# Seam of layers 0 and 1 batch by batch, and layer 1's scatters one a stage

## The chip, the cores and the metric

The kernel runs on one core of one Trainium2 chip. Its time is the device time of one execution in microseconds (us). The kernel before takes 1791.88 us in the median of three runs (1789.32 to 1793.81). The names of the engines are those of the profile: PE does matmuls and transposes (PEld loads their weights), DVE vector work, ACT activations and copies, POOL vector work and the indirect DMAs that it issues itself, SP issues the other DMAs.

## The reference, cut to what matters

A batch of 4 sequences of 512 tokens with 128 channels goes through four layers. In each, `x = x + s * silu(f)`, where `s` comes from a mixer and `f` from an expert network, and both read the normalized input.

```python
xn = layernorm(x)
s = mamba_block(xn)                # layer 0: selective scan, 256 inner channels, 16 states
g = silu(moe0(xn))                 # 8 experts, dense, weighted by the top 2
x = x + s * g                      # <- end of layer 0
xn = layernorm(x)                  # <- start of layer 1
s = layernorm(causal_attention(xn) @ w_proj + b_proj + xn) * gamma + beta   # 16 heads of 8
g = silu(moe1(xn))                 # 4 usable experts of 704 hidden units, top 2
x = x + s * g
# layers 2 and 3 follow in the same form
```

The two lines with arrows are the seam. Layer 1's attention looks only within a sequence, and a norm only at one token, so batch 0 of layer 1 needs nothing of batches 1 to 3. The routing of `moe1` is over all 2048 tokens: a token's place among those of its expert depends on all tokens before it.

## The kernel before, in words

A batch is 512 tokens, four rows of 128 tokens on the partitions (`NC` = 16 such chunks in all). `x`, `s` and `acc` hold all of them as `[128, 16, 128]`; `xnT` is the normalized input transposed, `[128 channels, 2048 tokens]`.

**Layer 0** (`layer0`, L573) runs a loop of 128 scans (L721 to L725) over 32 tiles of each batch. A step has the decay on ACT (L712, `dA`, made six steps ahead), the product `dBx` (L719) and the scan (L723) on DVE, the product with C on POOL (L725), and every four steps a sum over states on PE (L734). The experts' 32 steps, (expert, batch) in this order, lie between: the hidden matmul on PE (L558), GELU on ACT (L559), the output matmul on PE (L569), and the weighted add into `acc` on DVE (L519). The last expert's four steps finish `acc` for batches 0, 1, 2 and 3 one after the other. `back(b)` (L745 to L752) projects the scan's result of a batch into `s`; for the last batch this is the last work of the layer. `load_x` fetches `x` a second time near the end (L270), because four of its tiles serve as buffers of the scan.

**The seam**: `end_layer0` (L438) does one silu over all of `acc`, then `s = s * acc` and `x = x + s` in two halves. `begin_layer` (L431) takes `bn_stats` and `bn_aggr` of 16 chunks (L297, L298), one square root and reciprocal for all, 16 normalizes (L316), 16 transposes on PE (L323), and four copies into `xnT` (L324). POOL clears buffers of the attention meanwhile (L1701, L1707); SP loads the eight constant key blocks (L1704), then the attention's weights (L894, L896).

**Layer 1's attention** (`attention`, L882) runs in steps, one for each (batch, group of four heads, key block): 64 of them. Step k takes two score passes for a step 8 ahead (`first_pass`: PE L919 and L926, then the maximum of a row on DVE, L1026), and the two probability passes of its own (PE L919, exp on ACT L1057, and for the first 36 steps a causal mask on POOL, L1061). The matmuls with the values (`apply`, L1073) of step k - 1 stand between them. So steps -8 to -1 have score passes alone. `project(b)` (L962) makes queries, keys and values of a batch and splits q and k into bf16 parts; `spread(n)` (L1002) is 16 DMAs on SP that lay the parts of a group out for the passes. `shift` (L1028) sends the row maxima to the queries by four more DMAs.

**Routing** (`Routed.route`, L1200) is a generator. It takes the gate logits of all tokens (16 matmuls, L459), then some 40 small DVE operations, in which each token's two places in the experts' list are found, and then 32 scatters on POOL (L1298): chunk c of the rows goes to its first and to its second places in `xs` in HBM. After that `load` fetches two tiles' weights (L1311, 1.18 MB each, on POOL) and rows (L1317, on SP). Each scatter writes into the same `xs`, and in the order of instructions it waits for the semaphore of the scatter before it.

**What sets the order.** Within `tc.manual_schedule` an engine's instructions stay in the order in which the program makes them; the seam before is outside of it. The order in layer 1 is planned by `Places` (L334). Each attention step offers two stages (`place`, called in the middle and at the end of `step`). In a stage, due jobs go first (projections, shifts, ends of groups), then one stage of a due chain (`work`), and then, if a rule allows, one stage of the generator in `beside` (`aside`). What the generator yields says when it may go on:

```python
if self.needs == "free" or self.needs == "dve" and dve_left or self.needs is None and bank_left and (
    self.every or not second or not was
):
    self.aside()
```

`"free"` is any stage, `"dve"` the first of a step (and the second in every third step), and nothing means that a PSUM bank is needed. A chain that was served comes up again one step later (`gap=1`). `need(key)` runs a chain to its end at once. After step 35 (`PAUSE`) the rest of the routing is run, and then `routed.run` (L1342) does 19 tiles of experts, whose first hidden matmul is L1354.

`turn(b)` (L1406) is the seam's work for one batch, used so far behind layers 1 and 2: the product on POOL, the add, statistics and normalizes on DVE (`rows_norm`, L407, with Ln and Exp on ACT for the root), four transposes and a copy into `xnT`.

Of the kernel before, what the change touches and what calls it, by code (L numbers as in the profile page):

```python
# [11 lines left out]
F32 = mybir.dt.float32  # L12
BF16 = mybir.dt.bfloat16
I32 = mybir.dt.int32
AF = mybir.ActivationFunctionType
# [215 lines left out]
def kernel(ctx: ExitStack, tc: tile.TileContext, ap: dict):  # L231
# [34 lines left out]
    eps = cpool.tile([P, 1], F32, name="eps")  # L266
    dve.memset(eps, EPS)
# [23 lines left out]

    def norm_stats(src):

        st = small.tile([P, NC, 6], F32, tag="ln_st", name="ln_st")
        mv = small.tile([P, NC, 2], F32, tag="ln_mv", name="ln_mv")
        for c in range(NC):
            dve.bn_stats(out=st[:, c, :], in_=src[:, c, :])  # L297
            dve.bn_aggr(out=mv[:, c, :], in_=st[:, c, :])  # L298
        ve = small.tile([P, NC], F32, tag="ln_ve", name="ln_ve")
        dve.tensor_scalar(ve, mv[:, :, 1], EPS, None, ALU.add)  # L300
        sd = small.tile([P, NC], F32, tag="ln_sd", name="ln_sd")
        act.activation(sd, mv[:, :, 1], AF.Sqrt, bias=eps)
        r = small.tile([P, NC], F32, tag="ln_r", name="ln_r")
        dve.reciprocal(r, sd)

        t = small.tile([P, NC], F32, tag="ln_t", name="ln_t")
        dve.tensor_tensor(t, r, r, ALU.mult)
        dve.tensor_tensor(t, t, ve, ALU.mult)
        dve.tensor_scalar(t, t, -0.5, 1.5, ALU.mult, ALU.add)
        dve.tensor_tensor(r, r, t, ALU.mult)  # L310
        return mv, r

    def normalize(dst, src, stats=None, chunks=range(NC)):
        mv, r = stats or norm_stats(src)
        for c in chunks:
            dve.tensor_scalar(dst[:, c, :], src[:, c, :], mv[:, c, 0:1], r[:, c : c + 1], ALU.subtract, ALU.mult)  # L316
# [113 lines left out]

    def begin_layer(s):  # L431

        normalize(s, x)
        xnT = keep.tile([P, N], F32, name="xnT")
        transpose_chunks(xnT, s, NC)
        return xnT

    def end_layer0(s, y):  # L438

        act.activation(y, y, AF.Silu)  # L440
        half = NC // 2
        for h in range(2):
            cs = slice(h * half, (h + 1) * half)
            dve.tensor_tensor(s[:, cs, :], s[:, cs, :], y[:, cs, :], ALU.mult)
            dve.tensor_tensor(x[:, cs, :], x[:, cs, :], s[:, cs, :], ALU.add)
# [127 lines left out]
    def layer0(ctx0, mp, fp, s_out, acc):  # L573
# [31 lines left out]
        xnT = keep.tile([P, N], F32, name="xnT")  # L605
# [576 lines left out]
    class Routed:  # L1182
# [17 lines left out]
        def route(self):  # L1200

            rp, wp = self.rp, self.wp
# [93 lines left out]
            for c in range(NC):  # L1296
                for a in range(2):
                    pool.indirect_dma_start(  # L1298
                        out=self.xs[:, :], out_offset=self.at(a, c), in_=self.rows[:, c, :], in_offset=None,
                        bounds_check=TILES1 * SLOT1 - 1, oob_is_err=False,  # L1300
                    )
                    yield "free"
                    yield "free"
# [102 lines left out]
    def turn(b, s, y, xnT):  # L1406
# [4 lines left out]
        pool.tensor_tensor(sb, sb, yb, ALU.mult)  # L1411
# [273 lines left out]
    acc = keep.tile([P, NC, D], F32, name="acc")  # L1685

    with banks("l0", 0, True, bank=3, py=1, dBx=2, B=1, y=1):
        with tc.tile_pool(name="moe0", bufs=2) as fp, tc.tile_pool(name="mamba", bufs=1) as mp:
            with ExitStack() as ctx0:
                layer0(ctx0, mp, fp, s, acc)  # L1690
    end_layer0(s, acc)

    with banks("l1", 3, True, bank=1, py=1), tc.tile_pool(name="heads", bufs=1) as hp:
# [8 lines left out]
        for g in pads["k"]:  # L1702
            for t in g:
                nc.sync.dma_start(out=t, in_=ap["c_kb"])  # L1704

        for t in vaug:
            pool.memset(t[:, :, :, SUM : SUM + 1], 1.0)  # L1707
        xnT = begin_layer(s)

# [18 lines left out]
        with ExitStack() as to3, tc.manual_schedule(engines=engines):  # L1728
# [3 lines left out]
            with tc.tile_pool(name="moe1w", bufs=1) as wp:  # L1732
# [8 lines left out]
                a1 = attention(1, hp, None, xnT, pads, vaug, s, end1)  # L1741
                for _ in a1.first:
                    pass
# [91 lines left out]
```

## Time and profile before

| | |
|---|---|
| median of the runs | 1791.88 us |
| the profiled execution: its time, its span | 1787.83 us, 1786.1 us |
| mean granted PE clock | 0.835 |
| busy: PE, DVE, ACT, POOL | 1355.6, 1149.5, 954.2, 535.8 us |
| last matmul of layer 0 (L750) ends | 475.28 us |
| first projection of layer 1 (L968) starts | 491.81 us |
| first score matmul (L919) starts | 509.43 us |
| first mask (L1061, step 0) | 535.50 us |
| first and last scatter (L1298) start | 529.26, 646.65 us |
| first weights of the routed experts (L1311) | 648.59 us |
| first hidden matmul of the routed experts (L1354) | 669.76 us |

Times in the timeline count from the start of the span. A line of it gives start, length, engine, source line, operation, output and inputs, how many instructions were merged, and in brackets the idle time of the engine before it with what ended that. In the table by stages each engine has its busy time and the number of its instructions; PEclk is the granted clock as a share of full speed.

### The profile page before, as it was taken

The numbers are of one execution on the slowest core, as the hardware profiler recorded it, in microseconds if no ns is written. First come the engines' busy times: TensorE is split into PE (matmuls) and PEld (weight loads), VectorE is DVE, ScalarE is ACT, GpSimd is POOL, SyncE is SP. The second block draws the span as 40 slices with busy tenths as digits, with TensorE's granted clock in tenths as the row PEclk, the third lists the DMA queues.
The fourth block names the chain that finished last, engine by engine and source line by source line (L and its number), as shares of the span: only waits on it lengthen the run. The fifth ranks groups of instructions, "written<-read, shape, count | busy, mean of one in ns | idle before, by whom it ended". The sixth has DMA issues, their size and how long they took to land.

```text
span 1786.1 us, 22629 instructions
## 1 busy us (share of the span) xinstructions
PE 1355.6 (76%) x7845; PEld 690.0 (39%) x7845; DVE 1149.5 (64%) x2007; ACT 954.2 (53%) x1307; POOL 535.8 (30%) x513
## 2 busy tenths in 40 slices
PE   5588878887568889998687667876768876788771
PEld 2345545555333338886232122322313322233331
DVE  6378788787755653322586876567658799976322
ACT  3456656665325653222336767786884544365640
POOL 1236364554505651112543403114011101031223
PEclk8589989899757889999688878788888898898875
DMA  3567778488221132432212240311311211112112
GB/s 111 152 165 208 173 235 219 137 227 203 62 39 37 41 104 78 162 113 70 41 20 55 33 61 6 54 18 26 47 27 26 80 19 19 19 41 68 40 39 76
DMA packets 119923, 149.69 MB, mean 84 GB/s; under 512 B 14393, under 2 KB 80513, under 8 KB 118017
## 3 DMA queue, kind: packets, MB, share of 16 engines
q1 hardware_dynamic: 112848, 123.60, 29.6%
q0 software_dynamic: 6960, 24.65, 4.2%
q8 instruction: 62, 1.02, 0.2%
q14 instruction: 53, 0.43, 0.1%
HBM read 114.89 MB, written 16.01 MB: 73 GB/s over the span
## 4 chain that ended last, share of the span: by engine, by line
PE 41%; DVE 19%; ACT 16%; issue 10%; DMA 8%; POOL 3%; SPq 2%; another core or an unknown queue 1%; ACTq 0%; DVEq 0%; POOLq 0%
PE py L1073 6%; PE wide L919 6%; PE wide L1354 6%; PE bank L558 5%; ACT at L1057 5%; DMA rep<-ddd 3%; PE wide L926 3%; DVE nm L1026 3%; PE py L1334 3%; ACT ep L1021 3%; DVE den L1022 3%; PE py L569 2%; ACT dA L712 1%; PE wide L968 1%; DVE hs L723 1%
## 5 line engine op out<-in xcount | busy, mean ns | idle before, releaser
L1057 ACT ACTIVATE at<-wide 128x1024 f32<-128x1024 f32 (+3 forms) x384 | 352.6, 924 | 261.1 <-PE wide L926 170.2
L1026 DVE TENSOR_REDUCE nm<-wide 128x2 f32<-128x1024 f32 (+3 forms) x256 | 256.8, 1019 | 100.7 <-PE wide L926 86.9
L1073 PE MATMUL py<-at,vaug 128*32 128x512 f32 (+3 forms) x1536 | 235.7, 670 | 11.8 <-POOL at L1061 8.6
L725 POOL TENSOR_TENSOR hc<-hs,C 128x512 f32<-128x512 f32 x128 | 163.0, 1279 | 226.6 <-DVE hs L723 124.4
L1022 DVE TENSOR_REDUCE den<-ep 128x2 f32<-128x1024 f32 x128 | 155.4, 1217 | 114.3 <-ACT ep L1021 113.6
L919 PE MATMUL wide<-k,q 48*128 48x512 bf16 (+4 forms) x768 | 165.2, 407 | 78.2 <-ACT at L1057 43.4
L558 PE MATMUL bank<-xnT,w 128*128 128x512 f32 x256 | 142.0, 704 | 80.9 <-ACT h L559 53.6
L723 DVE TENSOR_TENSOR_SCAN hs<-dA,dBx 128x512 f32<-128x512 f32 x128 | 154.8, 1210 | 9.2 <-POOL hc L725 9.2
L1021 ACT ACTIVATE ep<-wide 128x1024 f32<-128x1024 f32 x128 | 132.8, 1037 | 43.5 <-PE wide L919 34.0
L926 PE MATMUL wide<-own_bf 128*128 128x128 bf16 x880 | 137.1, 243 | 0.0
L712 ACT ACTIVATE dA<-rep,A 128x512 f32<-128x512 f32 x128 | 86.7, 715 | 85.7 <-DMA rep<-ddd 47.7
L919 PE MATMUL wide<-q,k 63*128 63x512 bf16 (+3 forms) x512 | 100.4, 387 | 41.0 <-ACT at L1057 24.4
L569 PEld LDWEIGHTS py<-w,h 128*128 128x128 f32 x1024 | 120.2, 194 | 19.3 <-issue 9.8
L569 PE MATMUL py<-w,h 128*128 128x128 f32 x1024 | 121.8, 278 | 1.3 <-DVE acc L519 1.3
L558 PEld LDWEIGHTS bank<-xnT,w 128*128 128x128 f32 x256 | 54.3, 223 | 169.1 <-ACT h L559 75.8
L919 PEld LDWEIGHTS <-q 48*128 48x128 bf16 (+1 forms) x768 | 49.8, 96 | 162.3 <-issue 143.8
L1359 DVE TENSOR_TENSOR h<-h,wide 128x512 f32<-128x512 f32 x57 | 39.2, 688 | 110.2 <-ACT h L1357 110.2
L1354 PE MATMUL wide<-xT,w 128*128 128x256 f32 x456 | 108.4, 387 | 2.1 <-ACT h L1357 1.6
L559 ACT ACTIVATE h<-bank,cols 128x512 f32<-128x512 f32 x128 | 84.7, 687 | 33.9 <-PE bank L558 33.3
L919 PE MATMUL wide<-qr,kr 48*128 48x512 bf16 x256 | 60.7, 448 | 45.9 <-ACT ep L1021 40.8
L926 PEld LDWEIGHTS <-own_bf 128*128 128x128 bf16 x880 | 51.9, 100 | 110.6 <-issue 103.6
L919 PEld LDWEIGHTS <-k 63*128 63x128 bf16 x512 | 29.1, 94 | 166.3 <-issue 152.4
(324 smaller groups left out, 2157.8 us busy)
## 6 DMA issues: line engine op xcount, KB each, us to landing
rep<-ddd SPq DMA_DIRECT2D x128, 256.0 KB
dx<-ddd SPq DMA_DIRECT2D x80, 256.0 KB
x<-ddd SPq DMA_DIRECT2D x48, 256.0 KB
q<-parts SPq DMA_DIRECT2D x192, 48.0 KB
k<-parts SPq DMA_DIRECT2D x192, 48.0 KB
w<-in_f_w_dram SPq DMA_DIRECT2D x18, 256.0 KB
ddd<-dd POOLq DMA_DIRECT2D x8, 512.0 KB
w<-in_f_w_dram SPq DMA_DIRECT2D x32, 128.0 KB
```

The source lines that it names most:

```text
L558: pe.matmul(ph, w1[:, f * P : (f + 1) * P], self.xnT[:, tb * L : (tb + 1) * L], start=True, stop=True)
L569: pe.matmul(py[:, cs], h[:, f, cs], w2[:, f, :], start=(f == 0), stop=(f == 3))
L723: dve.tensor_tensor_scan(h, st[n]["dA"], st[n]["dBx"], 0.0, ALU.mult, ALU.add)
L725: pool.tensor_tensor(hc, h, batch[tiles[n][0]]["C"], ALU.mult)
L919: pe.matmul(ps[:, j, lo:hi], lhs[m][r, cs], rhs[m][r, lo:hi], start=True, stop=not own)
L926: pe.matmul(ps[:, j, cs], lhs_own, rhs_own, start=False, stop=True)
L1021: act.activation(e, ps, AF.Exp)
L1022: dve.tensor_reduce(s["den"][:, qc, 2 * m : 2 * m + 2], e, AX.X, ALU.add)
L1026: dve.tensor_reduce(s["nm"][:, qc, 2 * m : 2 * m + 2], ps[:, :, :hi], AX.X, ALU.max, negate=True)
L1057: act.activation(a[:, :, lo:], ps[:, :, lo:], AF.Exp)
L1073: pe.matmul(s["po"][32 * j : 32 * j + 32, lo:], vaug[b % 2][:, kc, 4 * g + j, :], a[:, j, lo:], start=kc == 0, stop=kc == 3,)
L1354: pe.matmul(ph[:, g, m * SLOT1 : (m + 1) * SLOT1], wk[:, f + g, m, :], self.x[k], start=True, stop=True)
```

## The change

The seam is taken apart by batches. Layer 0 ends with four silus on ACT, one for each batch. The seam's work of a batch is now `turn(b)`, as behind layers 1 and 2, each put in a chain of the planner; for batch 0 the product is on DVE, and `places.need((0, 0))` runs it at once, before the attention's first projection. Batches 1 to 3 come a stage at a time in the attention's first steps. `project` already asks for the end of the chain `(i - 1, b)` before it reads `xnT`. The routing waits, giving up stage after stage, until all four chains are over. In its loop of scatters one of the two yields is gone, so that a scatter is placed in each stage instead of every second. The eight loads of constant keys are now issued after the attention's two weights. The tile `xnT` is made once and shared by both layers. `norm_stats`, `normalize`, `begin_layer`, `end_layer0` and the tile `eps` are no longer used.

In the order of instructions that the build gives the changed kernel, silu 0 and 1 and the vector work of `turn(0)` stand among the last scans of layer 0 on ACT and DVE, and each Ln and each Exp of the four turns has a table load of its own in front of it. The engines' orders from the end of the first 36 steps on are those of before.

```diff
-    def begin_layer(s):
-        normalize(s, x)
-        xnT = keep.tile([P, N], F32, name="xnT")
-        transpose_chunks(xnT, s, NC)
-        return xnT
-    def end_layer0(s, y):
-        act.activation(y, y, AF.Silu)
-        half = NC // 2
-        for h in range(2):
-            cs = slice(h * half, (h + 1) * half)
-            dve.tensor_tensor(s[:, cs, :], s[:, cs, :], y[:, cs, :], ALU.mult)
-            dve.tensor_tensor(x[:, cs, :], x[:, cs, :], s[:, cs, :], ALU.add)
...
         def route(self):
+            while not places.over.issuperset((0, b) for b in range(B)):
+                yield "free"
             rp, wp = self.rp, self.wp
...
                         out=self.xs[:, :], out_offset=self.at(a, c), in_=self.rows[:, c, :], in_offset=None,
                         bounds_check=TILES1 * SLOT1 - 1, oob_is_err=False,
                     )
-                    yield "free"
                     yield "free"
...
-    def turn(b, s, y, xnT):
+    def turn(b, s, y, xnT, eng=pool):
         cs = slice(4 * b, 4 * b + 4)
         sb, xb, yb = s[:, cs, :], x[:, cs, :], y[:, cs, :]
-        pool.tensor_tensor(sb, sb, yb, ALU.mult)
+        eng.tensor_tensor(sb, sb, yb, ALU.mult)
...
+    xnT = keep.tile([P, N], F32, name="xnT")
...
-    end_layer0(s, acc)
+    for b in range(B):
+        act.activation(acc[:, 4 * b : 4 * b + 4, :], acc[:, 4 * b : 4 * b + 4, :], AF.Silu)
...
-        for g in pads["k"]:
-            for t in g:
-                nc.sync.dma_start(out=t, in_=ap["c_kb"])
...
-        xnT = begin_layer(s)
...
                 a1 = attention(1, hp, None, xnT, pads, vaug, s, end1)
+                for g in pads["k"]:
+                    for t in g:
+                        nc.sync.dma_start(out=t, in_=ap["c_kb"])
+                for b in range(B):
+                    places.add((0, b), turn(b, s, acc, xnT, dve if b == 0 else pool))
+                places.need((0, 0))
                 for _ in a1.first:
                     pass
```

More of the change, by code (lines that the diff above doesn't have):

```diff
@@ L265 @@
     ident_bf, mask_bf, diag_bf = own_bf[:, 0, :], own_bf[:, 1, :], own_bf[:, 2:, :]
-    eps = cpool.tile([P, 1], F32, name="eps")
-    dve.memset(eps, EPS)
     def load_x(b):
@@ L289 @@
     pick2 = cpool.tile([PARTS * E2, 3], F32, name="pick2")
[L292 to L316, printed above, removed]
     def transpose_chunks(dst, src, n, first=0):
@@ L570, in output, with layer0 @@
             return lambda: add_weighted(self.acc, py, self.cw, tb, e)
-    def layer0(ctx0, mp, fp, s_out, acc):
+    def layer0(ctx0, mp, fp, s_out, acc, xnT):
         w_in = mp.tile([P, 2 * INNER], F32, name="w_in")
@@ L604, in layer0 @@
         ysel = const("ysel").rearrange("p (m r) -> p m r", r=32)
-        xnT = keep.tile([P, N], F32, name="xnT")
         at, n = _COLS["A_log"]
@@ L1689 @@
             with ExitStack() as ctx0:
-                layer0(ctx0, mp, fp, s, acc)
-    end_layer0(s, acc)
+                layer0(ctx0, mp, fp, s, acc, xnT)
+    for b in range(B):
+        act.activation(acc[:, 4 * b : 4 * b + 4, :], acc[:, 4 * b : 4 * b + 4, :], AF.Silu)
     with banks("l1", 3, True, bank=1, py=1), tc.tile_pool(name="heads", bufs=1) as hp:
```

## The prediction

> **What bounds the kernel now.** I read the seam and the part of layer 1 up to the routed experts stage by stage: first the busy time of each engine by stage, then the timeline, then the scatters' own line. The stages are: last work of layer 0, norm and transposes, first projection, steps -8 to -1, steps 0 to 7, steps 7.5 to 23, and the rest up to the first expert matmul (L1354 at 669.76 us).
>
> ```profile
> core 0: us, PE busy (x) PEld busy (x) DVE busy (x) ACT busy (x) POOL busy (x), PEclk, DMA share, GB/s
> 468.00:476.00 8.00, 4.44 (x21) 3.25 (x16) 2.66 (x4) 2.89 (x2) 2.87 (x2) 0.79 0.00 0
> 476.00:496.80 20.80, 9.68 (x28) 5.64 (x28) 15.16 (x60) 2.55 (x5) 9.57 (x16) 0.59 0.24 72
> 496.80:509.40 12.60, 5.17 (x32) 5.19 (x33) 2.52 (x3) 6.90 (x9) 0.00 (x0) 0.61 0.16 23
> 509.40:535.50 26.10, 16.00 (x81) 6.92 (x81) 22.38 (x67) 1.85 (x3) 2.13 (x2) 0.50 0.33 54
> 535.50:564.00 28.50, 23.93 (x170) 8.42 (x168) 18.02 (x27) 17.74 (x27) 17.45 (x25) 0.85 0.11 25
> 564.00:623.60 59.60, 50.71 (x370) 19.57 (x374) 35.16 (x77) 34.47 (x52) 34.08 (x53) 0.79 0.22 45
> 623.60:669.80 46.20, 37.41 (x302) 14.75 (x301) 28.17 (x53) 26.20 (x40) 27.19 (x41) 0.87 0.38 104
> ```
>
> The seam proper is a DVE chain (15.2 of 20.8 us), steps -8 to -1 too (22.4 of 26.1), later PE leads. The timeline shows the seam's two ends:
>
> ```profile
> 475.31 0.69 DVE L751 TENSOR_TENSOR s<-bank,rows 128x512 f32<-128x512 f32 x1 [4.46 <-PE bank L750]
> ...
> 485.14 5.10 DVE L316 TENSOR_SCALAR s<-x,ln_mv,ln_r 128x128 f32<-128x128 f32 x16
> ...
> 491.81 3.73 PE L968 MATMUL wide<-xnT,wqk 128*128 128x512 f32 x4
> ```
>
> POOL's timeline in steps 11 to 18 shows what the scatters do to the queue that also masks the probabilities (L1061), which PE's apply (L1073) waits for:
>
> ```profile
> 578.00 1.00 POOL L1298 DMA_INDIRECT xs<-acc,pos  x1 [0.31 <-issue]
> 579.01 0.78 POOL L1061 TENSOR_SCALAR_AFFINE_SELECT at<-at 128x256 f32<-128x256 f32 x2
> 581.54 1.00 POOL L1298 DMA_INDIRECT xs<-acc,pos  x1 [1.75 <-DMA xs<-acc,pos]
> 582.55 0.78 POOL L1061 TENSOR_SCALAR_AFFINE_SELECT at<-at 128x256 f32<-128x256 f32 x2
> 584.56 1.00 POOL L1298 DMA_INDIRECT xs<-acc,pos  x1 [1.23 <-DMA xs<-acc,pos]
> 585.57 0.78 POOL L1061 TENSOR_SCALAR_AFFINE_SELECT at<-at 128x256 f32<-128x256 f32 x2
> 587.12 1.00 POOL L1298 DMA_INDIRECT xs<-acc,pos  x1 [0.77 <-DMA xs<-acc,pos]
> ```
>
> A scatter waits on POOL until the one before has landed, and POOL's queue stands meanwhile. This happens 14 times in 32 already, at one scatter a step. The pitch from scatter to scatter where it waits is 2.53 us at least (635.11 to 637.64), 3.61 at most, 3.02 in the mean of the 14: about 2.54 where SP sends no q or k spread, 3.0 to 3.5 while it does.
>
> **The change part by part.** The sum is made against the profiled run (1787.8 us, span 1786.1); its differences are then put on the median of 1791.9.
>
> *1. Seam, batch 0 at once.* Removed from the path: two x 1.22 adds, sixteen norm chains and sixteen normalizes, the copies. In the instruction order of the changed kernel batch 0's product, add, statistics and normalizes stand between the last scans of layer 0, where DVE is idle: 4.48 us before 446.92, and 1.38 before 440.62; the 3.3 us of adds and statistics fit there. After layer 0's last matmul (L750, end 475.28) only four transposes (1.15) and a copy (0.59) remain, and the load of wqk, which waits for the same end: 0.1 to issue and 2.75 to land (the k<-parts DMA on the chain of waits). It now stands ahead of the eight c_kb loads, so L968 starts about 3.0 us after L750 instead of 16.5: -13.5. POOL's memsets (475.48 to 483.0) come free at about the same time as the first values copy needs them; had that copy been earlier still, they would bind.
>
> *2. What layer 0's tail pays.* Two silus come early with two table loads each, Ln and Exp one each: ACT has six loads more there. Row: a load takes 1.28 us and the next activation starts 0.02 later (449.51, then 450.81). Ln and Exp with their loads end at about 449.8 (from 446.7, when the decay before them ends), DVE would be free at 448.74: 1.0 us of stall. The GELU column after silu 1 ends 1.7 us late (three lots of 1.28 and 0.6, less PE's slower start), so PE's L569 too. Against this POOL's yz (2.34 us at 469.64, with a DVE product beside it) is alone now: 1.27. Net +0.6, ends 0 to +4. Here the Trainium skill (ScalarE: Activation LUTs, What ACT_TABLE_LOAD costs) speaks against the change: it gives about 2.66 us for each switch, a drain included. By it the four loads ahead of the last GELUs cost 5.5 us more and the later ones some 4; the sum at the end would be about +33 instead of +23. No row shows a drain, so I take 1.28 and keep the rest for the range.
>
> *3. Batches 1 to 3 in stages.* Each is 0.69 (add, as L751), four x 0.44 (statistics), 0.17, four x 0.2, four x 0.34: 4.8 us of DVE, 14.3 for three. All three stand between the score reductions of steps -6 to -3, where DVE sets the pace. Taken away there is the routing's DVE work, 8.2 us (22.4 less 12.7 of reductions and 1.4 of shifts). So +6, ends 0 to +10. The six table loads and six small ACT operations (9.3 us) run on an ACT with 1.85 us busy in 26.1; the first is late only if DVE waits for it, and a reduction and the next batch's statistics lie between. The transposes stand in PE's queue ahead of later scores and wait for the normalizes: bubbles within the end of +10.
>
> *4. Routing later.* Its 16 gate matmuls leave the gap at 497, which was hidden, and its 8.2 us of DVE fall into steps 0 to 7: 18.0 of 28.5 us busy now, 26.2 then. It fits as a sum, not at every place: +4, ends 0 to +8. So far -13.5 + 0.6 + 6 + 4 = -2.9 at step 7.5.
>
> *5. Scatters, one a stage.* In the instruction order they run from mask 15 to mask 46 of POOL's 72: steps 7.5 to 23, one scatter after each mask instead of one after two. Each still waits for the one before. What is queued behind a waiting scatter is the next mask; PE's apply waits for that, and, with three buffers of probabilities, ACT. So the region lasts 31 pitches. At two scatters per 5 us or more, a spread (6 us in every 4 steps) now touches two pitches of eight: (2 x 3.26 + 6 x 2.54)/8 = 2.72; 31 x 2.72 = 84.3. Two pitches also hold batch 2's q,k subtraction (2.13 + 0.43 + 1.0 on POOL) and its two parts (2.3 + 1.4): +2.8; stalls at the batch boundary, in which POOL's chain stops too: +1. Sum 88.1 against 59.6 today, +28.5. Ends: all pitches 2.53 and nothing more, 78.4: +19; 3.3 and the extras, 106: +46. The skill's price (DMA: Bandwidth & Descriptors, Anatomy of one DMA) for a transfer from this queue, 2.0 us plus bytes over 436 GB/s, would be 2.15 for 64 KB, 67 + 3.8 for the region, +11 instead of +28.5, the total about +6. The trace has no pitch under 2.53, so the rows decide.
>
> *6. After the last scatter.* Weights for two tiles are fetched 12 steps before the experts rather than 3.5. Today they land while batch 2's last spread does, and the split of batch 3 waits for that (the chain shows 7.85 us of DMA q<-parts at 651.58). Then it finds a quiet queue: some 2 us gained; the spread that now meets the weights has four steps to land. Steps 24 to 35 are free of scatters but PE leads there. SP's two loads of xs rows move up and stand ahead of a spread. -2, ends -6 to +3. Behind the experts nothing moves.
>
> Total: -13.5 + 0.6 + 6 + 4 + 28.5 - 2 = +23.6, that is 1791.9 + 23.6 = **1815.5 us**.
>
> **The rivals.**
> *A. The seam is given back (13 in 100).* Tail and stages at their upper ends: table loads of 2.66 (+5), stages +10, routing +8: instead of -2.9 about +10, total +37, 1829. For it: DVE is 86% busy in steps -8 to -1; against: no row has a drain.
> *B. The region is milder (18).* Pitch 2.53 throughout and no cost of stages beyond +2 and routing +1: -9.9 + 19 - 3 = +6, 1798. For it: the quiet pitches are 2.53 to 2.56. Against: the batch boundary.
> *C. Faster (7).* The chain of scatters stops binding, at L1298 on POOL. With the rest as summed, break-even is 31 p + 3.8 = 59.6 + 2.9 + 2, p = 1.96 us. At p = 1.6 the region is 53.4, -11: 1781. For it: the issue itself takes only 1.0 us. Against: all 14 waits.
> *D. No effect (4).* Gain and loss cancel, or steps so seldom reach POOL's wait that the doubled rate is hidden: 1792. Against: 8.9 us of waiting in this region at half the rate.
>
> **How the numbers follow.** My own case has 58 in 100 (1804 to 1828 for itself), with A, B, C, D 13, 18, 7, 4. A and B are slower, as is my own: slower 0.89, faster 0.07, same 0.04 (0.3%, 5.4 us, is about what a measurement of this kernel can tell). Leaving out C, D's lower half and the far end of A, the range is 1794 to 1835.
>
> **What would show it.** After: L968 starts about 13 us earlier after a tail of layer 0 about as long; the reductions of steps -8 to -1 take about 32 us; L1298 waits on the DMA before it nearly 31 times, first to last 88 us apart; PE L1073 waits for POOL L1061 in that region, and PE's busy share falls from 85% to under 60%; L1354 starts at about 693 us. It is wrong if the scatters' pitch is under 2.2 us, if steps 7.5 to 23 still take about 60 us, or if L1354 starts before 670.

## The result

The changed kernel takes 1807.97 us in the median (1801.17 to 1826.05), the kernel before 1791.88 us (1785.62 to 1798.70). The ratio is 1.0105, with a 95% interval of 1.0070 to 1.0141: slower, by 18.8 us at the ratio (the two medians alone are 16.1 us apart). The prediction was 1815.5 us. The profiled execution took 1811.83 us with a span of 1810.1, that is 24.0 us more than the one before.

Below, "after" is the changed kernel. Its lines are called by its own numbers: the mask is L1016 (L1061 before), the scatter L1255 (L1298), apply L1028 (L1073), the first expert matmul L1310 (L1354), the last matmul of layer 0 L705 (L750), the first projection L923 (L968), the gate matmuls L415, the score reduction L981, the q,k split L905 to L909, the two loads of gathered rows on SP L1273. In the other kernels below some of these numbers are one or a few higher.

The first view is after's busy time by stage, cut at the same events as before: last work of layer 0, transposes and first projection, wait for the first spread, steps -8 to -1, steps 0 to 7, steps 7.5 to 23, and the rest up to the first expert matmul (692.32 us).

```profile
core 0: us, PE busy (x) PEld busy (x) DVE busy (x) ACT busy (x) POOL busy (x), PEclk, DMA share, GB/s
468.00:475.20 7.20, 4.65 (x30) 2.86 (x24) 1.97 (x5) 0.63 (x1) 4.07 (x4) 0.85 0.00 0
475.20:481.50 6.30, 5.13 (x16) 2.72 (x14) 0.00 (x0) 1.68 (x4) 6.30 (x12) 0.63 0.70 209
481.50:494.00 12.50, 0.00 (x0) 0.10 (x1) 2.79 (x3) 6.67 (x8) 1.92 (x4) 0.57 0.15 23
494.00:530.30 36.30, 24.95 (x119) 14.53 (x119) 26.04 (x80) 11.11 (x17) 1.84 (x3) 0.50 0.26 42
530.30:557.40 27.10, 23.43 (x176) 9.57 (x174) 21.30 (x61) 17.47 (x28) 11.72 (x19) 0.92 0.05 8
557.40:645.97 88.57, 65.77 (x383) 21.93 (x384) 44.95 (x92) 35.53 (x53) 49.34 (x67) 0.74 0.19 45
645.97:692.70 46.73, 36.62 (x287) 14.49 (x284) 24.04 (x47) 26.18 (x39) 20.57 (x34) 0.83 0.35 90
```

The row to see is the sixth. The 31 masks from the 16th to the 47th took 59.5 us before and take 88.6 now, with 383 matmul records against 370, so on nearly the same work. The fourth row has grown too (26.1 before), while the two rows ahead of it have shrunk (18.8 us together, 33.4 before). The ends of the seam on PE:

```profile
471.82 2.24 PE L705 MATMUL bank<-w_out,yz 128*128 128x128 f32 x14 [1.76 <-POOL yz L698]
474.85 1.12 PE L1373 MATMUL bank<-cst,s 128*128 128x128 f32 x4 [0.78 <-DVE s L706]
476.85 3.47 PE L923 MATMUL wide<-xnT,wqk 128*128 128x512 f32 x4 [0.88 <-DMA wqk<-in_a_qk_dram]
```

The projection starts 2.8 us after layer 0's last matmul (474.06) instead of 16.5, and what it waits for last is its weights. POOL's timeline inside the sixth row, to be read beside the same view of before in the prediction:

```profile
571.17 0.99 POOL L1255 DMA_INDIRECT xs<-acc,pos  x1 [1.09 <-DMA xs<-acc,pos]
572.17 0.42 POOL L1016 TENSOR_SCALAR_AFFINE_SELECT at<-at 128x256 f32<-128x256 f32 x1
573.69 0.99 POOL L1255 DMA_INDIRECT xs<-acc,pos  x1 [1.09 <-DMA xs<-acc,pos]
...
576.21 0.99 POOL L1255 DMA_INDIRECT xs<-acc,pos  x1 [1.10 <-DMA xs<-acc,pos]
577.21 0.43 POOL L1016 TENSOR_SCALAR_AFFINE_SELECT at<-at 128x256 f32<-128x256 f32 x1
579.53 0.99 POOL L1255 DMA_INDIRECT xs<-acc,pos  x1 [1.90 <-DMA xs<-acc,pos]
```

One mask passes between two scatters, where two passed before, and the pitch is 2.51 us where a spread has hardly begun (571.17 to 573.69, 26 of its DMA packets), 3.32 where it is under way (576.21 to 579.53, 135 packets). Of the waited pitches 17 are of 2.50 to 2.55 us, with at most 87 such packets in each; of the ten longer ones eight have 135 or more, and two, of 2.90 and 3.19, have six and none and stay unexplained. For the scatters' own line, what POOL sat idle for, with the time and the number of instances, after and then before:

```profile
L1255 POOL DMA_INDIRECT xs<-acc,pos x32: 986/986/1098, 556.3 to 645.0; - x32
  DMA xs<-acc,pos: 34.5, 27
```

```profile
  DMA xs<-acc,pos: 16.3, 14
```

27 of 32 wait for the one before (14 before). PE's apply is where it arrives. The costliest PE group between 557 and 646 us, last column the idle time ahead of it, then the same group of before between 564.0 and 623.6 us:

```profile
L1028 PE MATMUL py<-at,vaug 128*32 128x128 f32 (+3 forms) x128 | 27.5, 600 | 17.2 <-POOL at L1016 17.1
```

```profile
L1073 PE MATMUL py<-at,vaug 128*32 128x128 f32 (+3 forms) x124 | 16.3, 549 | 2.2 <-POOL at L1061 2.2
```

Its idle time went from 2.2 to 17.2 us and its busy time from 16.3 to 27.5. The means mix four shapes. A lower granted clock in the region (0.74 for 0.79) and eight matmuls that ran as one block and now often run as two blocks of four, each behind a mask, go with the longer busy time; how much is due to each is not separated.

Stage by stage against the prediction's steps, in us of the profiled executions:

| stage | before | after | change | predicted |
|---|---|---|---|---|
| end of layer 0's last matmul | 475.28 | 474.06 | -1.2 | +0.6 |
| from there to the first score | 34.15 | 19.95 | -14.2 | -13.5 |
| first score to mask 1 | 26.1 | 36.3 | +10.2 | +6 |
| mask 1 to mask 16 | 28.5 | 27.1 | -1.4 | +4 |
| mask 16 to mask 47 | 59.5 | 88.6 | +29.0 | +28.5 |
| mask 47 to first expert matmul | 46.2 | 46.35 | +0.1 | -2 |
| sum | | | +22.5 | +23.6 |

Behind the first expert matmul the two instruction streams are the same; that part took 1116.4 us before and 1117.8 after. In the other profiles below it is 1104 to 1130 us where it has no edit of its own. One profiled execution is therefore good for stages and not for a total within some 13 us; totals are taken from the ratios, and the 5 us between +24.0 (profiles) and +18.8 (ratio) are not assigned to a stage. The ratios leave out executions more than 1.5% above the fastest of their kernel; the profile of 48 scatters is of such a one (a span of 1843.5 us at a mean clock of 0.805), so only its stages are used.

### The profile page after: what moved, and what is told of

It reads as the page before. It is cut to its first block, busy times and chain, and to the rows that moved or that the text cites. A ratio compares the mean times of both kernels' runs of the same rounds, so it can differ in the third digit from the quotient of the medians.

```text
span 1810.1 us, 22655 instructions
## 1 busy us (share of the span) xinstructions
PE 1383.3 (76%) x7845; PEld 694.7 (38%) x7845; DVE 1151.8 (64%) x2019; ACT 970.3 (54%) x1329; POOL 540.8 (30%) x516
## 4 chain that ended last, share of the span: by engine, by line
PE 40%; DVE 19%; ACT 15%; issue 11%; DMA 8%; POOL 5%; SPq 1%; another core or an unknown queue 1%; POOLq 0%; ACTq 0%; DVEq 0%
PE wide L874 6%; PE py L1028 6%; PE wide L1310 5%; PE bank L514 5%; ACT at L1012 4%; DMA rep<-ddd 3%; PE wide L881 3%; PE py L1290 3%; DVE den L977 3%; DVE nm L981 3%; ACT ep L976 2%; PE py L525 2%; POOL xs L1255 1%; ACT dA L667 1%; DVE hs L678 1%
## 5 line engine op out<-in xcount | busy, mean ns | idle before, releaser
L981 DVE TENSOR_REDUCE nm<-wide 128x2 f32<-128x1024 f32 (+3 forms) x256 | 257.1, 1018 | 122.9 <-PE wide L881 114.0
L1028 PE MATMUL py<-at,vaug 128*32 128x512 f32 (+3 forms) x1536 | 249.7, 682 | 28.6 <-POOL at L1016 22.3
L874 PE MATMUL wide<-k,q 48*128 48x512 bf16 (+4 forms) x768 | 169.6, 417 | 80.1 <-ACT at L1012 41.1
L680 POOL TENSOR_TENSOR hc<-hs,C 128x512 f32<-128x512 f32 x128 | 163.5, 1283 | 225.5 <-DVE hs L678 122.5
L514 PE MATMUL bank<-xnT,w 128*128 128x512 f32 x256 | 148.6, 732 | 76.0 <-ACT h L515 50.1
L1310 PE MATMUL wide<-xT,w 128*128 128x256 f32 x456 | 108.8, 388 | 2.1 <-ACT h L1313 1.6
L874 PEld LDWEIGHTS <-k 63*128 63x128 bf16 x512 | 28.8, 95 | 166.9 <-issue 150.0
```

The source lines that it names most:

```text
L514: pe.matmul(ph, w1[:, f * P : (f + 1) * P], self.xnT[:, tb * L : (tb + 1) * L], start=True, stop=True)
L680: pool.tensor_tensor(hc, h, batch[tiles[n][0]]["C"], ALU.mult)
L874: pe.matmul(ps[:, j, lo:hi], lhs[m][r, cs], rhs[m][r, lo:hi], start=True, stop=not own)
L981: dve.tensor_reduce(s["nm"][:, qc, 2 * m : 2 * m + 2], ps[:, :, :hi], AX.X, ALU.max, negate=True)
L1028: pe.matmul(s["po"][32 * j : 32 * j + 32, lo:], vaug[b % 2][:, kc, 4 * g + j, :], a[:, j, lo:], start=kc == 0, stop=kc == 3,)
L1310: pe.matmul(ph[:, g, m * SLOT1 : (m + 1) * SLOT1], wk[:, f + g, m, :], self.x[k], start=True, stop=True)
```

## The experiments

Theory S says: the seam gains a little, and the loss is the doubled rate of the scatters, each of which stands on POOL until the one before it has landed. Theory T says: the loss is in the stages of the turns and in the later routing. In the table, each ratio is to the kernel before on the same chip; "path" is from layer 0's last matmul to the first expert matmul, "chain" from the first scatter to the last, "wait" POOL's idle time for the scatter before, all from the profiles.

| kernel | median | before | ratio, 95% | path | chain | wait |
|---|---|---|---|---|---|---|
| before | | | | 194.5 | 117.4 | 16.3 |
| after | 1807.97 | 1791.88 | 1.0105 (1.0070 to 1.0141) | 218.3 | 88.7 | 34.5 |
| seam alone | 1792.29 | 1786.86 | 1.0028 (1.0007 to 1.0049) | 209.9 | 115.6 | 17.6 |
| scatters alone | 1809.70 | 1786.86 | 1.0122 (1.0082 to 1.0162) | 224.8 | 87.8 | 37.8 |
| two chains | 1778.72 | 1786.86 | 0.9954 (0.9931 to 0.9977) | 194.7 | 62.8 | 1.0 |
| three stages for two | 1789.96 | 1786.86 | 1.0006 (0.9981 to 1.0031) | 207.3 | 100.1 | 27.3 |
| 48 scatters | 1833.29 | 1797.07 | 1.0176 (1.0105 to 1.0246) | 238.0 | 132.5 | 53.0 |
| gate in parts | 1818.20 | 1797.07 | 1.0127 (1.0077 to 1.0177) | 225.3 | 87.2 | 35.1 |
| masks on PE | 1811.23 | 1797.07 | 1.0098 (1.0064 to 1.0132) | 214.9 | 85.5 | 46.7 |
| two joined chains | 1792.51 | 1797.07 | 0.9981 (0.9953 to 1.0009) | 196.7 | 64.8 | 0.8 |
| POOL cleared | 1803.25 | 1786.03 | 1.0083 (1.0058 to 1.0108) | 217.7 | 88.0 | 57.7 |
| gate in parts, early | 1802.75 | 1786.03 | 1.0089 (1.0063 to 1.0115) | 216.6 | 88.2 | 36.5 |
| joined chains, gate in parts | 1776.23 | 1786.03 | 0.9946 (0.9924 to 0.9968) | 196.0 | 64.1 | 1.5 |
| half rows | 1794.37 | 1786.03 | a single time | 215.2 | 84.8 | 31.6 |

### The two halves of the change, each alone

The seam alone: after, with the place between two scatters that the change removed put back.

```diff
                     pool.indirect_dma_start(
                         out=self.xs[:, :], out_offset=self.at(a, c), in_=self.rows[:, c, :], in_offset=None,
...
                     yield "free"
+                    yield "free"
```

> The changed kernel with the second yield after each scatter put back (one scatter a step, as before): the seam alone. Theory S (the doubled rate of the scatters costs the time, the seam itself gains): masks 15 to 47 take about 60 us again instead of 88.6, the first projection, step 0 and mask 15 stay where the changed kernel has them (about 15, 5 and 7 us earlier than before). But the routing starts 13 steps later, so some three scatters and the weights of the first tiles are left for the end of step 35: 8 us of scatters and 10 to 13 us of weights before the first expert matmul. Sum -7 + 0 + 15: about 1800 us. Theory T (the stages of batches 1 to 3 and the late routing cost the time): masks 15 to 47 stay near 80 us or more and the time stays at 1808 or above.

The scatters alone: before, with that place taken away (the opposite line, a removed `yield "free"`).

> The kernel before with one of the two yields after a scatter taken out: the scatters' rate alone, the seam as it was. Theory S: the region from the first to the last scatter has 31 pitches of 2.6 to 3.0 us, 80 to 93 us, and covers steps -1 to 15, which took 65 us before: +18 to +26, of which some 2 us come back later because the weights arrive early: 1808 to 1816 us. Theory T: 1792 us, no change, since the seam is not touched.

The doubled rate alone has a ratio of 1.0122, as much as the whole change, and its median lies in the range that theory S gave. Its chain lasts 87.8 us like after's, though it starts at another point (530.3 us, ahead of mask 1) and lies beside other steps. Theory T is out as the carrier of the loss: this kernel has neither turns in stages nor a late routing.

The seam alone brings no gain on the clock, and is slower by 0.3% (about 1800 us was expected; it is 1792.3). The trace shows where the gain goes. At mask 47 it is 5.3 us ahead of before, counted from layer 0's last matmul, at mask 72 level with it, and then the experts wait, as POOL's and PE's timelines have it:

```profile
668.97 0.97 POOL L1255 DMA_INDIRECT xs<-acc,pos  x1 [1.52 <-DMA xs<-acc,pos]
...
672.92 0.99 POOL L1268 DMA_INDIRECT w<-in_f_w_dram,expert  x1 [0.30 <-issue]
```

```profile
678.67 0.66 PE L1281 MATMUL bank<-cst,xr 128*128 128x128 f32 x2 [15.10 <-DMA xr<-xs]
679.84 3.78 PE L1311 MATMUL wide<-xT,w 128*128 128x256 f32 x8 [0.52 <-DVE xT L1283]
```

Routing that ends later (first scatter at 553.4 us, 529.3 before) shifts a chain of 115.6 us so far back that its last scatter comes after the last mask (662.45), and PE waits 15.1 us for the gathered rows. Of these 15 us the ratio shows 5; in this profile layer 0 ends 5.4 us earlier than in before's, and the part behind the first expert matmul is 5.8 us shorter, which is within what single executions of such kernels differ by. So the change's two halves are bound together: a late start of the chain asks for a denser chain, and the denser chain stops POOL.

### Taking the chain away, thinning it, lengthening it

Two chains: second places go to another buffer in HBM, whose rows nothing reads, so a scatter waits only for the one before the last.

```diff
+            self.xs2 = dram.tile([TILES1 * SLOT1, D], F32, name="xs2")
...
-                        out=self.xs[:, :], out_offset=self.at(a, c), in_=self.rows[:, c, :], in_offset=None,
+                        out=(self.xs, self.xs2)[a][:, :], out_offset=self.at(a, c), in_=self.rows[:, c, :], in_offset=None,
```

> The changed kernel with the scatters of the second places sent to a second buffer in HBM that nothing reads, so that a scatter waits for the one two before it and not for the one before. The number of scatters, their size, their places in the order and all other work are kept; left out of the computation are the second experts' rows, which stay zero. Theory S: waiting for the DMA before a scatter falls from 34.5 us to under 8, masks 15 to 47 take 60 to 66 us, and the time is 1783 to 1792 us, below the kernel before. Theory T: waits fall, but the time stays at 1805 to 1812.

```profile
L1256 POOL DMA_INDIRECT xs<-acc,pos x32: 986/987/1098, 554.9 to 617.7; - x32
  issue: 5.6, 28
  DMA xs<-acc,pos: 1.0, 3
```

The same 32 transfers, at the same places, of the same size; only the wait of each for its predecessor is gone, 1.0 us of 34.5 being left. Mask 16 to mask 47 takes 62.65 us instead of 88.6, and the kernel is faster than before (0.9954; a little more than the 1783 to 1792 us expected). PE is busy for 51.6 us of it at a granted clock of 0.86, where it was 65.8 at 0.74, so the longer busy time of after goes with the wait. The bytes and the issue on POOL (0.99 us each) are not the cost; the wait is.

Three stages for two scatters: a place after every second scatter (`if a: yield "free"` added).

> The changed kernel with a second yield after every second scatter: four scatters in three steps. Theory S: 1.33 scatters a step at 2.75 us are 3.7 us a step, about what steps 7 to 30 took before with their other work; masks 15 to 61 take about 88 us against 84 before, and with the seam's -7 the time is 1786 to 1792 us, the kernel before or a little less. Theory T: 1805 or more.

It lies between the two rates: 22 waits, 27.3 us, a chain of 100.1 us. The ratio, 1.0006, is the kernel before, as S expected, but the stage was missed: masks 15 to 61 took 99.6 us, not 88 (84.0 before). That the time came out all the same is not explained by this profile, whose path is 12.8 us longer than before's.

48 scatters: each chunk's first scatter is sent twice (`for a in (0, 0, 1)`), the same rows to the same slots.

> The changed kernel with three scatters per chunk of rows instead of two (the first one is sent twice, same rows to the same slots): 48 scatters, still one a stage, so the chain runs from mask 15 to mask 62 instead of to mask 46. Nothing else is changed. Theory S (every stage that holds a scatter lasts one pitch of the chain): the 16 stages from mask 47 on lasted 1.55 to 1.66 us each without a scatter and would last about 2.8, so 18 to 20 us more than the changed kernel (1808), first scatter to last about 133 us, time about 1827. Theory T (the loss is in the stages of the seam and in the late routing): the extra scatters cost nothing that can be measured, 1808.

In the profile the chain takes 132.5 us, 2.82 a pitch, and mask 47 to mask 61 takes 40.0 us instead of 23.2; from mask 16 to the first expert matmul it is 154.5 us against 134.9, +19.6, which is what S expected. The ratio (1.0176) is above after's 1.0105, but the interval is wide and the two meet. Masks 16 to 47, which have the same scatters in both kernels, took 87.4 us there and 88.6 in after, so the 19.6 us lie where the added scatters are.

Half rows: the scatters write 64 of the 128 elements of each row. The rest of every gathered row is left out, so the experts compute on other data.

```diff
-                        out=self.xs[:, :], out_offset=self.at(a, c), in_=self.rows[:, c, :], in_offset=None,
+                        out=self.xs.rearrange("n (k d) -> (n k) d", k=2), out_offset=self.at(a, c), in_=self.rows[:, c, : D // 2], in_offset=None,
```

> The changed kernel whose 32 scatters each write only the first half of every row (64 of 128 elements, 32 KB instead of 64, at half the stride), so the experts read other data than the reference asks for. If the pitch of the chain is the time of a transfer's bytes, the quiet pitch falls from 2.52 to about 1.4 to 1.9 us and the region from mask 16 to 47 from 88.6 to 60 to 68 us. If it is the fixed time of issuing, landing and reporting one transfer, the pitch stays at 2.3 us or more and the region at 80 us or more.

```profile
569.45 0.99 POOL L1255 DMA_INDIRECT xs<-acc,pos  x1 [1.01 <-DMA xs<-acc,pos]
570.45 0.43 POOL L1016 TENSOR_SCALAR_AFFINE_SELECT at<-at 128x256 f32<-128x256 f32 x1
571.88 0.99 POOL L1255 DMA_INDIRECT xs<-acc,pos  x1 [1.00 <-DMA xs<-acc,pos]
```

The quiet pitch is 2.43 us instead of 2.51: half the bytes save 0.08 us. So the pitch is not the time of the bytes. The packet records of the trace show the same: in a quiet pitch of after the packets of a scatter lie between 1.57 and 1.88 us from its start (1.57 and 1.81 here), and 2.2 of the 2.51 us are ahead of them or behind them. Each transfer still has 128 rows, so whether the part ahead depends on their number is not shown. The Trainium skill (DMA: Bandwidth & Descriptors, Anatomy of one DMA) gives 2.0 us plus the bytes at 436 GB/s for one transfer; by that 32 KB more are 0.075 us, an estimate, and the measured 0.08 agrees. Its 2.15 us for 64 KB, an estimate too, is to be held against the landing and not against the pitch: where the trace records a landing in a quiet pitch, it comes 2.27 us after the scatter's start (pitch 2.54, scatters alone; with half rows 2.17 and 2.43), and some 0.27 us more pass before the next scatter starts. For a chain the measured pitch decides.

### What stands behind a scatter

Masks on PE: the causal mask of steps 7 to 29 is added to the scores by two more matmuls a pair, which later steps do anyway, so no mask stands behind a scatter.

```diff
-            late = causal and 4 * n + kc >= PAUSE
+            late = causal and (4 * n + kc >= PAUSE or 7 <= 4 * n + kc < 30)
```

> The changed kernel with the causal mask of steps 7 to 29 added by TensorE (the two extra 128x128 matmuls per pair that steps 36 and later have already) instead of being cut by GpSimd after the exponential. The scatters keep their rate, their order and their waits, but no mask stands behind them on GpSimd's queue. Theory S with the mask as the carrier (apply waits for the mask, the mask for the scatter): mask-less stages run at TensorE's pace, mask 16 to mask 61's place takes 85 to 97 us instead of 112, the time is 15 to 25 us below the changed kernel although TensorE does 13 us more work (46 pairs at 0.29); apply no longer waits for GpSimd. If the scatters hold the kernel in another way (their transfers against the spreads, or the q,k split behind them on GpSimd), the time stays within 5 us of the changed kernel or above it.

The gain did not come (1.0098). PE ran on for 47 us of the chain and then stood still. Windows of 16 us, then PE's and POOL's timelines:

```profile
589.00:605.00 16.00, 14.59 (x134) 7.28 (x132) 9.29 (x18) 7.41 (x12) 5.82 (x6) 1.00 0.16 40
605.00:621.00 16.00, 0.00 (x0) 0.00 (x0) 0.00 (x0) 1.65 (x2) 8.47 (x8) 0.58 0.06 25
```

```profile
622.62 0.64 PE L1028 MATMUL py<-at,vaug 128*32 128x128 f32 x4 [18.67 <-ACT at L1012]
```

```profile
616.20 0.97 POOL L1255 DMA_INDIRECT xs<-acc,pos  x1 [1.52 <-DMA xs<-acc,pos]
617.18 2.14 POOL L905 TENSOR_TENSOR qk<-qk,parts 128x1024 f32<-128x1024 f32 x1
```

The stages had run ahead of the chain, and the q,k split of batch 2, which stands on POOL's queue behind 23 scatters, came through at 617.2 us. ACT waited 19.4 us for it, PE behind ACT 18.7. This is the other reading that the expectation named.

POOL cleared: the same, with batch 2's split and the row addition after batch 0's attention on DVE.

```diff
-            alone = i == 1 and b == 0
+            alone = i == 1 and b in (0, 2)
...
-                pool.tensor_tensor(sb, sb, row("b_proj1"), ALU.add)
+                (pool if b else dve).tensor_tensor(sb, sb, row("b_proj1"), ALU.add)
```

> As the kernel with the masks of steps 7 to 29 on TensorE, and besides the q,k split of batch 2 and the row addition after batch 0's attention moved from GpSimd to VectorE, so that nothing which another engine waits for stands behind a scatter; the scatters keep rate, order and waits. In the kernel with the masks alone TensorE stood still from about 605 to 621 us, until the split of batch 2 (617.2 us) had come through behind 23 scatters. Theory S, widened (a scatter's wait costs whatever stands behind it on GpSimd's queue and is needed, mask or split): the hole is gone, the first expert matmul comes 15 to 20 us earlier than with the masks alone (688 us there), and the time is 15 to 25 us below the changed kernel. If the scatters hold the kernel by their transfers (the spreads wait for the DMA queues), the hole stays and the time is within 5 us of the kernel with the masks alone.

A miss again: 1.0083, and the first expert matmul, which was to come 15 to 20 us earlier, starts no earlier (path 217.7 against 214.9). That hole is gone, and another stands some 35 us later. PE's timeline, the waits of SP's queue (total, number, longest), and SP's timeline:

```profile
661.02 0.42 PE L874 MATMUL wide<-k,q 48*128 48x128 bf16 x2 [20.50 <-DMA k<-parts]
```

```profile
SPq L1273 <- DMA xs<-acc,pos: 23.7, 1, 23.7
```

```profile
648.81 0.90 SPq L1273 DMA_DIRECT2D xr<-xs  x2
649.81 3.05 SPq L964 DMA_DIRECT2D q<-parts  x4
652.91 2.87 SPq L964 DMA_DIRECT2D k<-parts  x4
```

SP's two loads of gathered rows wait 23.7 us for the last scatter, and the next spread of q and k stands behind them on SP. PE waits for that spread. With the masks, the split and the row addition off POOL, the chain held the kernel through the queue of another engine. In all of after, masks on PE and POOL cleared, 32 scatters take 85.5 to 88.7 us; whatever is needed and stands behind them, on POOL or on SP, comes when the chain lets it. The transfers themselves did not hold the spreads: the spread at 615 to 625 us went through in the middle of the chain.

### The gate matmuls

After's profile has the 16 gate matmuls (32 records) in one block of 6.9 us at a granted clock of 0.50 (5.2 us in before, in a gap that hid them), and a score reduction behind it, on PE's and on DVE's timeline:

```profile
520.29 6.93 PE L415 MATMUL bank<-gates,xnT 128*128 128x4 f32 x32
```

```profile
528.13 1.23 DVE L981 TENSOR_REDUCE nm<-wide 128x2 f32<-128x1024 f32 x1 [5.93 <-PE wide L881]
```

In parts: the four columns of a batch as soon as its turn is over.

```diff
-            while not places.over.issuperset((0, b) for b in range(B)):
-                yield "free"
...
+                while (0, q) not in places.over:
+                    yield "free"
+                pv = bank()[:, : 4 * E1].rearrange("p (c e) -> p c e", e=E1)
+                for c in range(4):
...
+                yield
```

> The changed kernel with the routing's gate logits taken in four parts: as soon as a batch's turn is over its 4 columns of gate matmuls, the copy of its logits and of its rows are placed, one part a place, instead of all 16 after the fourth turn. The changed kernel shows those 32 passes as one block of 6.9 us on TensorE at a granted clock of 0.50, and the score reduction after it waits 5.9 us for TensorE. If the block is on the path, score passes to mask 1 take 30 to 33 us instead of 36.3 and the time is 3 to 6 us below the changed kernel. If VectorE sets the pace there anyway, the time stays within 1 us of it. The scatters' region is as in the changed kernel (88 us from mask 16 to mask 47) in both cases.

The score passes took 34.1 us instead of 36.3 (30 to 33 were expected), steps 0 to 7 took 34.2 instead of 27.1, and the sum is a loss. The routing started one place later and its top-2 met POOL's split. DVE of this kernel, then POOL of this kernel, then DVE of after:

```profile
543.94 2.37 DVE L447 TENSOR_TENSOR t<-t,cst 128x256 f32<-128x256 f32 x1
```

```profile
543.90 2.12 POOL L905 TENSOR_TENSOR qk<-qk,parts 128x1024 f32<-128x1024 f32 x1 [0.28 <-ACT parts L904]
```

```profile
536.56 0.51 DVE L447 TENSOR_TENSOR t<-t,cst 128x256 f32<-128x256 f32 x1
```

An operation of 0.51 us lasts until POOL's has ended (546.31 and 546.02). The Trainium skill (SBUF — State Buffer, Who interferes with whom) says that a DVE instruction with two SBUF inputs contends with a GpSimd instruction that reads SBUF, and that the port pair which they share is an exclusive lock; this row agrees. All six top-2 operations took 5.4 us (542.94 to 548.39) instead of 2.4. PE idled behind DVE, and its granted clock fell:

```profile
546.00:550.00 4.00, 1.23 (x10) 0.41 (x7) 3.90 (x6) 3.30 (x4) 3.38 (x5) 0.75 0.00 0
550.00:554.00 4.00, 1.16 (x6) 0.34 (x5) 3.69 (x13) 2.07 (x4) 0.82 (x2) 0.50 0.00 0
554.00:558.00 4.00, 4.00 (x26) 2.23 (x26) 1.64 (x6) 1.19 (x2) 0.00 (x0) 0.50 0.00 0
```

In parts, early: the routing one place earlier (`yield None if q < 3 else "dve"` after a part), which restores after's order on DVE.

> The gate logits in four parts as before, but the routing's VectorE work starts one place earlier, which puts VectorE's instructions into the same order as in the changed kernel. With the four parts alone the score passes took 34.1 us instead of 36.3, but steps 0 to 7 took 34.2 instead of 27.1: the six top-2 operations then ran beside GpSimd's q,k split (one of them took 2.37 us instead of 0.51) and TensorE's granted clock fell to 0.50 while it waited. If that meeting is the cause: top-2 as short as in the changed kernel, steps 0 to 7 about 27 us again, 2 to 4 us below the changed kernel in all. If the gate block was no cost of its own: the passes to mask 1 still take 34 us or steps 0 to 7 grow by what they lose, and the time is that of the changed kernel.

The top-2 operation is back at 0.51 us, steps 0 to 7 take 28.8 us, the passes 34.1. The loss came with the later place and went with it. The meeting itself shows 3.0 of the 7.1 us, in the six operations; the edit moved all of the routing's DVE work, so the other 4 us, part of them the lower clock, are not separated. The net gain is small: 2.2 less 1.7 us in the profile, 1.0089 against 1.0105 on the clock, which the intervals do not separate (2 to 4 us were expected). So the block's own price is 2.2 us of the 5.9 that the reduction waited: in the passes DVE waits 16.0 us for PE in after and 13.8 here, the same PE work being there in smaller pieces.

### A version faster than both

Two joined chains: the second buffer is kept and zeroed in layer 0, the experts load both rows of a tile, and POOL adds them one tile ahead.

```diff
+                for to, xs in zip(self.x[k], self.xs):
+                    nc.sync.dma_start(
+                        out=to, in_=xs[k * SLOT1 : (k + 1) * SLOT1, :].rearrange("(h p) d -> p h d", p=P)
+                    )
...
+        def joined(self, k):
+            first, second = self.x[k]
+            pool.tensor_tensor(first, first, second, ALU.add)
+            self.x[k] = first
```

> The changed kernel with two chains of scatters that keep their meaning: the first places go to one buffer in HBM, the second places to another, both zeroed in layer 0; the experts load both rows of a tile and GpSimd adds them before the transposes (19 more zero transfers, 19 more loads, 19 adds of about 0.65 us). Theory S: as with the two chains whose second half was not read (mask 16 to 47 in about 62 us, 27 to 29 us below the changed kernel), less what the joining costs; the adds and loads lie beside TensorE, which sets the experts' pace, so 22 to 29 us below the changed kernel and 3 to 8 us below the kernel before. If the joining is on the path (a tile's transposes wait for the add), the experts' part grows by up to 19 x 0.65 = 12 us and the time is about that of the kernel before or above it. Theory T: no gain over the changed kernel.

It keeps most of what two chains gain: 64.7 us from mask 16 to 47, ratio 0.9981, which is 22 us below after by the two ratios, at the lower end of what was expected. Against before, where 3 to 8 us were expected, it cannot be told from no change. Mask 72 to the first expert matmul takes 3.7 us instead of 2.2, the first tile's join.

Joined, with the first join seven stages after its loads and the gate in parts with the early start:

> Two chains of scatters into two zeroed buffers with the join on GpSimd, as before, with the join of the first tile placed seven stages after its loads instead of ahead of the first expert, and with the gate logits in four parts with the early start. If the three effects add up: 1.5 us less before the first expert, 2 to 4 us less in the seam, so 6 to 9 us below the kernel before; if the gate parts bring nothing, 3 to 5 us below it.

```profile
497.68:531.74 34.06, 23.19 (x111) 12.77 (x111) 26.32 (x81) 11.40 (x19) 1.84 (x4) 0.50 0.25 39
531.74:559.24 27.50, 23.87 (x176) 9.62 (x174) 21.15 (x61) 17.54 (x28) 11.75 (x19) 0.87 0.05 8
559.24:623.17 63.93, 51.02 (x374) 19.29 (x374) 38.71 (x85) 34.61 (x52) 49.28 (x67) 0.84 0.23 58
```

Steps -8 to -1, steps 0 to 7 and the scatters' region, in after's cuts: 34.1, 27.5 and 63.9 us against 36.3, 27.1 and 88.6. The time is 1776.23 us against 1786.03, ratio 0.9946: 9.6 us faster than before by the ratio (6 to 9 were expected), and this is the only complete version that is clearly faster. In the profiles its path (196.0) is not shorter than before's (194.5), so the gain on the clock cannot be placed in a stage from one execution of each.

## Why the prediction was right, point by point

The direction, the place and the mechanism held, and 1808.0 lies inside 1794 to 1835. The value was 7.5 us too high against the median; against the profiles, on which the sum was made, +23.6 stands beside +24.0. That agreement is partly luck, since the terms below were off both ways.

Step 1, the seam (-13.5), held: 2.8 us from L705's end to L923, and -14.2 at the first score. As said, the load of wqk is what ends last.

Step 2, the tail (+0.6), cannot be told from nothing: -1.2 in the two profiles, while the kernels with this same tail end it between 469.8 and 478.1 us. The weighing against the 2.66 us for a table switch of the Trainium skill (ScalarE: Activation LUTs, What ACT_TABLE_LOAD costs) came out for the row: a load lasts 1283 ns in every group of after, ACT sits idle for 0.1 us at most ahead of each group's loads between 400 and 700 us, and the next activation starts 0.02 us behind a load (447.25, then 447.27). The extra 10 us that a drain would have given, by the prediction's estimate, are absent from the sum.

Step 3, batches in stages (+6, ends 0 to +10), was mis-sized: it measured +10.2. The step left out a term. It noted in step 4 that the gate matmuls "leave the gap at 497, which was hidden", but did not ask where they land: behind the fourth turn, at half clock, where DVE waits for the scores behind them. Nor did DVE alone set the pace: its busy time in the stage grew by 3.7 us, not 6, and its idle time by 6.6, of which the one wait behind the gates is 5.9. Taken in parts the gates give 2.2 us back; the other 2.0 of the miss are not assigned.

Step 4, later routing (+4), was too dear: -1.4. The routing's 8.2 us fit between the reductions. The fit depends on one place more or less, since steps 0 to 7 took 7 us more when the routing came one place later and met POOL's split.

Step 5, the scatters (+28.5), held: +29.0, first to last 88.7 us against 88.1 said. Its parts held too: the 27 waited pitches are 2.75 us in the mean (2.72 said), and the four others exceed that by 3.3 us in all (3.8 said). Two chains, scatters alone, 48 scatters and half rows each confirm a part of it: that the wait is the cost, that the rate alone is enough, that it grows with the number, that the bytes are little of the pitch. What it named as the carrier, the mask behind the scatter, is the first of three and not the only one: the split and SP's loads take its place when the mask is gone.

Step 6, after the last scatter (-2), did not show: +0.1.

Rival A (the seam is given back) did not come: at mask 16 after is 6.6 us ahead, where -2.9 was the sum. Rival B (a milder region) is the nearest of the rivals on the clock, 1798 against 1808, but its mechanism failed: the pitch was 2.86 in the mean, not 2.53. Rival C needed the region below 64.5 us (a pitch of 1.96 and 3.8 us of extras); two chains reach 62.65, and that kernel is faster. Rival D (no effect) is excluded by the interval.

Of the signs named ahead, L968's start (15.0 us earlier), the 88 us of the chain, apply's wait for the mask and L1354's start (692.3) came as said. The passes took 36.3 us, not about 32. One sign was wrong: PE's busy share in the region is 74% (65.8 of 88.6), not under 60%: busy time grew from 50.7 to 65.8 us on nearly the same work, with a lower granted clock and longer records of L1028; with two chains it is 51.6 again. A PE that is held up can look busy. "Nearly 31" waits were 27.

## What to carry to other kernels

A chain of dependent transfers has a least length of its own, here 31 pitches of 2.76 to 2.86 us in the mean, however densely the program places it; compare that with the time until its result is needed, before spreading it thinly (it ends late) or densely (its queue stops). A wait at the head of an in-order queue is charged to whatever needed work stands behind it, on that queue and on any queue that waits for the chain's end: moving one consumer away uncovers the next, so break the dependence instead, here by two buffers and one addition. When work is moved out of a hidden gap, cost the place where it lands, too, with that place's clock and with what runs beside it on other engines.

## What was not expected of the hardware

PE's granted clock is 0.50 through all of steps -8 to -1 in before and after alike, though from 518 to 534 us of after PE was busy for 15.65 of 16 us, and the gates that were moved there took 6.9 us instead of 5.2. With the gate in parts, a PE busy for 1.2 of 4 us had 0.75 in those 4 us and 0.50 in the next, and then, in full use, 0.50 and 0.55 for eight more before it had 1.00 again. A DVE operation of 0.51 us took 2.37 beside a POOL operation of 2.12. Halving the bytes of a scatter changed its pitch by 0.08 of 2.51 us. And Ln and Exp in direct succession had a table load of 1.28 us each (five and five between 400 and 700 us).
